# Seven block products instead of eight for the down projection of 24 experts rather than 13, with the outgoing-row buffers shared out anew

## The chip, the cores and the metric

The kernel runs on one core of a Trainium2 chip. The metric is the time of one execution on the device, in microseconds (us). It is the median of several runs.

The core's engines work side by side, each through its own instructions in program order, and semaphores tie them together: TensorE (PE, matrix products; its weight loads are shown apart as PEld), VectorE (DVE), ScalarE (ACT), GpSimd (POOL, which here issues the gathers and scatters of token rows) and SyncE (SP, which issues the plain transfers).

## The reference

The reference is a cross-attention followed by a mixture of experts, on 16 x 128 = 2048 tokens of 512 values:

```python
x = x + xattn(layernorm(x), ctx_512, ctx_512)
h = layernorm(x).reshape(2048, 512)
tidx, tw = gate(h, gate_weight, e_bias)             # 8 of 32 experts for a token
comb = zeros((2048, 32)).at[rows, tidx].set(tw)
g = einsum('td,eid->tei', h, w1)                    # w1, w3: (32, 256, 512)
u = einsum('td,eid->tei', h, w3)
a = silu(g) * u
routed = einsum('tei,edi,te->td', a, w2, comb)      # w2: (32, 512, 256)
shared = silu(h @ sw1.T) * (h @ sw3.T) @ sw2.T
out = x + routed + shared
```

All data are float32. What matters here is the last product of an expert, its down projection: a block of tokens with 256 activations each, times the expert's 256 x 512 matrix `w2`, then scaled by the token's weight for this expert and added to the token's row of the output.

## The kernel before

**The stages.** The first 225 us hold attention, the gate, the routing of tokens to experts and most of the shared expert. The rest, to the end of the span at 863.5 us, goes through the 32 routed experts one after the other. The change lies in this part.

**Places and slices.** `ORDER` lists the experts (by rank of their load), `CAPS` gives each its number of places, and `begins[k]` is the first place of the k-th. All places together are 17664, or 138 slices of 128 (`NS`). For every slice j, GpSimd gathers 128 token rows (`gather`, L1455), VectorE turns them in 32x32 blocks (`transpose`, L1496), and copies (L1493) put the blocks in place as `xall`, tokens along the free dimension.

**Up.** Experts 1 to 30 are `fast`: their up products, for `w1` and `w3`, are made by `seven(k)`, a Winograd scheme that makes a 2x2 block product from seven products (L1598) instead of eight. VectorE makes the sums of weights (L1560), of tokens (L1589) and of products (L1608); ScalarE and VectorE make silu and the product into `acts_of` (`sa`). An expert with over 512 rooms goes in two halves of seven steps each (14 steps); a smaller one in one pass of seven steps.

**Down.** Two ways exist. `down(j)` makes one slice in full: two products of 128x512 a slice (L1739), each shown as two records, into a PSUM tile of its own (`ps_y` or `ps_z`). `evict` then scales it on ScalarE into a row tile `yw` (L1755), and `send_all` has GpSimd scatter it to the output, adding (L1711). A slice that holds places of two experts is sent twice, the second time with the next expert's first send.

`seven_downs(k)` makes four whole slices of one expert at once, as a 2x2 block product of 512 tokens by 512 outputs over 256: seven block products (L1821), each two products of 128x256, into the PSUM pool `ps_p` with its six banks, which the up products use too. It is a generator of eight steps. The first makes four sums on VectorE (L1854); the next seven make one block product each. VectorE makes four more sums of 128x256 and five of 128x512 (both L1812), ScalarE one copy (L1858) and six scalings (L1833). The rows leave in two pair tiles `yp` of two slices each. Its sums lie in the memory of the shared expert's weights (`sup`, `sdn`), one copy of each.

`four_of(k)` decides between the two: it gives the first of four whole slices of expert k, or nothing. Before the change it gives nothing for an even k. So the 13 odd experts from 1 to 25 go through `seven_downs` (52 slices), and the other 86 slices through `down`.

**The order.** All engines but SP run in the order in which the program is written (`manual_schedule`). The main loop goes over half experts (`pieces`), step by step. In every step it first emits the up product, then the jobs that came due (`tick`; `soon(f, after)` puts them on a later step), then a share of the turning, copying and sums by their planned costs, and then so many units of down work as `planned` says: a plain slice weighs 2, a step of `seven_downs` weighs 1. The four first sums of `seven_downs(k)` are emitted three steps into expert k+1; its products follow the units ahead of it, with a rest of four weights kept for the next half.

**Order of sends.** The additions of expert k+1 to the output wait for the landing of those of expert k (`tc.add_manual_dep` in `send`), because both may hold the same token. GpSimd waits in order, and gathers stand behind.

Of the kernel before, what the change touches and what calls it, by code (L numbers as in the profile page):

```python
# [9 lines left out]
F32 = mybir.dt.float32  # L10
# [8 lines left out]
P = 128  # L19
# [27 lines left out]
def tile_xattn_moe(  # L47
# [16 lines left out]
    B, S, D = x.shape  # L64
    E, _, ND, I = w1.shape
# [991 lines left out]
    def experts(ups, in_order, later, products):  # L1057
# [18 lines left out]
        for k in range(E + 1):  # L1076
            r = min(k, E - 1)
# [27 lines left out]
        def load_weights(k, up, down):  # L1105

            r = k % NW
            with tc.issue_after(last[0]) if last else nullcontext():
                _, (e,) = nc.values_load_multi_w_load_instructions(
                    order[0:1, k : k + 1],  # L1110
                    engines=[mybir.EngineType.SP],
                    min_val=0,
                    max_val=E - 1,
                    skip_runtime_bounds_check_because="experts' numbers",
                    bass_reorder=False,
                )
            both = [(wup[r][:, 0], w1), (wup[r][:, 1], w3)] if up else []
            if down:
                both.append((wdn[r], w2))
            for dst, src in both:  # L1120
                dma = nc.sync.dma_start(
                    dst, src[bass.ds(e, 1)].rearrange("o p a b -> (o p) a b")
                )
            last[:] = [dma.ins]
# [317 lines left out]
        def experts_at(j):  # L1442

            for k in range(E):
                a, b = max(begins[k], j * P), min(begins[k + 1], (j + 1) * P)
                if a < b:
                    yield k, a - j * P, b - j * P, a - begins[k]

        xg, yws = {}, {}
# [67 lines left out]
        def soon(f, after=1):  # L1517
            jobs.setdefault(now + after, []).append(f)
# [211 lines left out]
        def down(j):  # L1730
# [19 lines left out]
                    load_weights(ks[0] + NW, False, True)  # L1750
            soon(lambda: evict(j, y))

        def evict(j, y):
            yws[j] = late.tile([P, D], F32, tag="yw", name="yw", bufs=4)
            nc.scalar.activation(yws[j], y, AF.Copy, scale=wt[:, j : j + 1])  # L1755
            send_all(j)

        def send_all(j):
            for args in waiting:
                send(*args)  # L1760
            waiting.clear()
            rows_of = {k: (a, b) for k, a, b, _ in experts_at(j)}
            ks = sorted(rows_of)
            send(j, ks[0], *rows_of[ks[0]])
            waiting.extend((j, k, *rows_of[k]) for k in ks[1:])

        def fast(k):
            return 0 < k < E - 1

        def four_of(k):  # L1770

            if k % 2 == 0 or not fast(k):
                return None
            j = -(-begins[k] // P)
            return j if (j + 4) * P <= begins[k + 1] else None
# [5 lines left out]
        def seven_downs(k):  # L1781


            j = four_of(k)
            first, second = range(j, j + 2), range(j + 2, j + 4)
            col = j * P - begins[k]
            a11, a12, a21, a22 = (
                acts_of[k % NA][:, i, c : c + 2 * P] for c in (col, col + 2 * P) for i in range(NI)
            )
            b11, b12, b21, b22 = (  # L1790
                wdn[k % NW][:, i, c : c + DH] for i in range(NI) for c in (0, DH)
            )
            t1, t2, t3, t4, s1, s2, s4 = (sums_at[:, i] for i in range(7))
            s3 = a21
            p1, u2 = temps_at[:, 0], temps_at[:, 1]
            pending = []

            def then(f, after=1):
                def once():
                    if once in pending:  # L1800
                        pending.remove(once)
                        f()

                pending.append(once)
                soon(once, after)

            def settle():
                for f in list(pending):
                    f()

            def sum_of(to, a, b, op, after=1):
                then(lambda: nc.vector.tensor_tensor(to, a, b, op), after)  # L1812

            def bank():
                return ps_p.tile([P, TB], F32, tag="p", name="y").rearrange(
                    "p (r t) -> p r t", r=2
                )

            def times(acc, a, b, first=True):
                for r in range(2):  # L1820
                    nc.tensor.matmul(  # L1821
                        acc[:, r, :],
                        lhsT=a[:, ts(r, P)],
                        rhs=b,
                        start=(first and r == 0),
                        stop=(r == 1),
                        skip_group_check=not first,
                    )

            def scaled(to, of, js, after):  # L1830
                for r, at in enumerate(js):
                    then(
                        lambda r=r, at=at: nc.scalar.activation(  # L1833
                            to[:, r], of[:, r], AF.Copy, scale=wt[:, at : at + 1]
                        ),
                        after,
                    )

            def sent_out(rows, js, after):
                for r, at in enumerate(js):  # L1840

                    def f(r=r, at=at):
                        yws[at] = rows[:, r, :]
                        send_all(at)

                    then(f, after)

            for to, a, b, op in (
                (s1, a21, a22, ALU.add),
                (s2, s1, a11, ALU.subtract),  # L1850
                (t1, b12, b11, ALU.subtract),
                (t2, b22, t1, ALU.subtract),
            ):
                nc.vector.tensor_tensor(to, a, b, op)  # L1854
            yield
            pa = bank()
            times(pa, a11, b11)
            then(lambda: nc.scalar.copy(p1, pa))  # L1858
            yield
            rows1, rows2 = (late.tile([P, 2, D], F32, tag="yp", name="yp") for _ in range(2))  # L1860
            settle()
            times(pa, a12, b21, first=False)
            scaled(rows1[:, :, 0:DH], pa, first, 1)
            for to, a, b in ((t3, b22, b12), (s3, a11, a21), (s4, a12, s2), (t4, b21, t2)):
                sum_of(to, a, b, ALU.subtract)
            yield
            pb = bank()
            times(pb, s2, t2)
            sum_of(u2, p1, pb, ALU.add)
            yield  # L1870
            pc = bank()
            times(pc, s1, t1)
            sum_of(rows2[:, :, DH:], u2, pc, ALU.add)
            yield
            pd = bank()
            settle()
            times(pd, s3, t3)
            sum_of(rows2[:, :, DH:], rows2[:, :, DH:], pd, ALU.add)
            yield
            times(pc, s4, b22, first=False)  # L1880
            sum_of(rows1[:, :, DH:], u2, pc, ALU.add)
            scaled(rows1[:, :, DH:], rows1[:, :, DH:], first, 3)
            sent_out(rows1, first, 3)
            yield
            settle()
            times(pd, a22, t4, first=False)
            sum_of(rows2[:, :, 0:DH], u2, pd, ALU.add)
            scaled(rows2, rows2, second, 3)
            sent_out(rows2, second, 3)
            if (j + 4) * P == begins[k + 1] and k + NW < E:  # L1890
                load_weights(k + NW, False, True)
            yield
# [3 lines left out]
        def units(j0, j1, ready):  # L1896


            j, of = j0, []
            while j < j1:  # L1900
                ks = [k for k, *_ in experts_at(j)]
                if len(ks) == 1 and four_of(ks[0]) == j:
                    steps = seven_downs(ks[0])
                    jobs.setdefault(ready, []).append(lambda steps=steps: next(steps))
                    of += [(lambda steps=steps: next(steps), ready, 1)] * 7
                    j += 4
                else:
                    of.append((lambda j=j: down(j), ready, 2))
                    j += 1
            return of  # L1910
# [42 lines left out]
        late = ctx.enter_context(tc.tile_pool(name="late", bufs=2, side="right"))  # L1953
# [16 lines left out]
        for n in range(len(pieces)):  # L1970
            k = pieces[n][0]
# [91 lines left out]
    pieces = [(k, i) for k in range(NTB) for i in range(NI)]  # L2063
    left_over = attention_small()
    experts(pieces[1:], in_order, *left_over)
    left = nc.values_load(
        more[0:1, 0:1],
# [63 lines left out]
```

## Time and profile before

| what | value |
|---|---|
| median of 3 runs | 866.39 us (865.27 to 867.35) |
| the profiled execution | 865.3 us; span 863.5 us; mean granted TensorE clock 0.997 |
| busy: PE, DVE, ACT, POOL | 849.7 (98%), 652.6 (76%), 641.2 (74%), 473.5 us (55%) |
| chain that ended last | PE 96%, POOL 2%, ACT 1% |
| down products in that chain | L1739 (plain slices) 16%, L1821 (seven products) 9% |
| scalings into `yw`, L1755 | 86 |
| scalings into `yp`, L1833 | 78 (26 each of three kinds) |
| scatters, L1711 | 98 from `yw`, 52 from `yp` |

How to read it: busy time of an engine is the time covered by its instructions; the records of one engine can overlap by some tens of ns, so the distance from start to start says what an instruction costs in a stream. The chain is followed back from the last instruction, at each step to what released it.

### The profile page before, as it was taken

What the parts mean: (1) busy time and instruction counts of PE and PEld (TensorE: products, weight loads), DVE (VectorE), ACT (ScalarE), POOL (GpSimd) and SP (SyncE); (2) the same over time, 40 slices, a digit from 0 to 9 for tenths busy, and PEclk for the clock granted to TensorE, in tenths of its full rate; (3) what the DMA queues carried; (4) which work ended last, traced back from release to release, by engine and by line L of the source; (5) the groups of instructions that cost most, each with busy time, mean ns of one, the idle gap of its engine ahead of it and who ended that gap; (6) DMA issues with size and microseconds to landing.
All of it is one profiled execution on the core that took longest, in us unless ns stands there. A gap on an engine that the chain in (4) does not pass through costs nothing.

```text
span 863.5 us, 13499 instructions
## 1 busy us (share of the span) xinstructions
PE 849.7 (98%) x4171; PEld 568.3 (66%) x4171; DVE 652.6 (76%) x1593; ACT 641.2 (74%) x1156; POOL 473.5 (55%) x588
## 2 busy tenths in 40 slices
PE   8999999999999999999999999999999999999995
PEld 5344444555766776767686767686778878887763
DVE  7877778858877797778797979797878888867410
ACT  5889741628987797788887979787888888977831
POOL 4487560034545666555646656666564555466554
PEclk9999999999999999999999999999999999999998
DMA  9111111647576888678878878787787788778554
GB/s 293 78 38 49 63 50 44 238 128 214 147 186 128 199 183 215 167 153 188 200 199 159 220 150 224 171 215 166 199 163 203 159 194 204 155 213 164 86 88 57
DMA packets 59873, 137.14 MB, mean 159 GB/s; under 512 B 12168, under 2 KB 16392, under 8 KB 59792
## 3 DMA queue, kind: packets, MB, share of 16 engines
q0 software_dynamic: 32032, 69.25, 42.2%
q1 hardware_dynamic: 27680, 66.81, 23.0%
q8 instruction: 35, 0.57, 0.3%
q14 instruction: 46, 0.38, 0.1%
q10 hardware_dynamic: 80, 0.13, 0.1%
HBM read 96.71 MB, written 46.73 MB: 166 GB/s over the span
## 4 chain that ended last, share of the span: by engine, by line
PE 96%; POOL 2%; issue 1%; ACT 1%; DMA 0%; DVE 0%; POOLq 0%; ACTq 0%
PE p L1598 45%; PE y L1739 16%; PE y L1821 9%; PE gu L285 6%; PE sc L492 5%; PE oT L508 4%; PE y L1392 3%; PE x L462 2%; PE gu L1528 2%; PE tok L1043 1%; POOL out_dram L1711 1%; PE lgT L569 0%; PE lg L584 0%; DMA out_dram<-yw,token 0%; ACT p L502 0%
## 5 line engine op out<-in xcount | busy, mean ns | idle before, releaser
L1493 ACT COPY xall<-blocks 32x512 f32<-32x512 f32 (+4 forms) x684 | 360.4, 527 | 16.3 <-DVE blocks L1496 6.6
L1711 POOL DMA_INDIRECT out_dram<-yw,token x98 | 157.0, 1602 | 138.2 <-DMA out_dram<-yw,token 38.3
L1455 POOL DMA_INDIRECT xgs<-rows,token x138 | 152.8, 1107 | 125.8 <-DVE token L1055 54.2
L1598 PE MATMUL p<-xall,wup 128*128 128x270 f32 (+27 forms) x720 | 185.7, 393 | 0.0
L1598 PEld LDWEIGHTS p<-xall,wup 128*128 128x128 f32 x720 | 136.6, 190 | 38.1 <-issue 10.9
L1739 PE MATMUL y<-wdn,sa 128*128 128x512 f32 (+2 forms) x464 | 161.4, 595 | 0.0
L1598 PE MATMUL p<-t,s 128*128 128x270 f32 (+27 forms) x480 | 123.8, 394 | 0.0
L1711 POOL DMA_INDIRECT out_dram<-yp,token x52 | 85.0, 1635 | 69.2 <-ACT yp L1833 46.4
L1755 ACT ACTIVATE yw<-y,wt 128x512 f32<-128x512 f32 x86 | 58.9, 685 | 72.5 <-PE y L1739 61.1
L1598 PEld LDWEIGHTS p<-t,s 128*128 128x128 f32 x480 | 91.1, 190 | 28.4 <-issue 11.1
L1496 DVE STREAM_TRANSPOSE blocks<-xgs 128x512 f32<-128x512 f32 x138 | 97.2, 705 | 7.7 <-DMA xgs<-rows,token 7.6
L1739 PEld LDWEIGHTS y<-wdn,sa 128*128 128x128 f32 (+2 forms) x464 | 61.4, 162 | 54.7 <-issue 48.2
L1608 DVE TENSOR_TENSOR z<-u,p 128x270 f32<-128x270 f32 (+27 forms) x96 | 48.7, 507 | 42.8 <-PE p L1598 40.2
L502 ACT ACTIVATE p<-sc 128x1024 f32<-128x1024 f32 x64 | 62.1, 1024 | 13.6 <-PE sc L492 13.6
L1598 PE MATMUL p<-t,wup 128*128 128x270 f32 (+27 forms) x240 | 63.8, 396 | 0.0
L1598 PE MATMUL p<-xall,s 128*128 128x270 f32 (+27 forms) x240 | 63.4, 394 | 0.0
L285 PE MATMUL gu<-xall,sup 128*128 128x512 f32 x128 | 59.2, 602 | 0.0
L1598 PEld LDWEIGHTS p<-t,wup 128*128 128x128 f32 x240 | 45.0, 190 | 18.3 <-issue 8.6
L1598 PEld LDWEIGHTS p<-xall,s 128*128 128x128 f32 x240 | 45.3, 190 | 14.3 <-issue 3.1
L1608 DVE TENSOR_TENSOR u<-u,p 128x270 f32<-128x270 f32 (+27 forms) x48 | 24.4, 507 | 30.4 <-PE p L1598 19.4
L492 PE MATMUL sc<-qT,kz 32*128 32x512 f32 x256 | 44.2, 639 | 0.5 <-ACT p L502 0.2
L1589 DVE TENSOR_TENSOR t<-xall,t 128x540 f32<-128x540 f32 (+27 forms) x60 | 43.5, 725 | 1.0
(241 smaller groups left out, 1218.6 us busy)
## 6 DMA issues: line engine op xcount, KB each, us to landing
wup<-in_w_dram SPq DMA_DIRECT2D x64, 512.0 KB
wdn<-in_w_dram SPq DMA_DIRECT2D x32, 512.0 KB
rows<-xn SPq DMA_DIRECT2D x16, 256.0 KB
out_dram<-x SPq DMA_DIRECT2D x16, 256.0 KB
x<-in_x_dram SPq DMA_DIRECT2D x15, 256.0 KB
xgs<-rows,token POOLq DMA_INDIRECT x138
out_dram<-yw,token POOLq DMA_INDIRECT x98
cTs<-in_cT_dram SPq DMA_DIRECT2D x4, 256.0 KB
```

The source lines that it names most:

```text
L285: nc.tensor.matmul(acc, lhsT=sup[:, w, d, ts(i, P)], rhs=xnT[k][:, d, :], start=(d == 0), stop=(d == ND - 1),)
L492: nc.tensor.matmul(scs[j // 2][:, j % 2], lhsT=kzs[b // 4 % 2][rows, b % 4, i, :], rhs=qT[rows], start=True, stop=True, tile_position=(j * ...
L502: nc.scalar.activation(p, sc, AF.Exp, scale=1.0 / HD**0.5)
L1455: nc.gpsimd.indirect_dma_start(out=t, out_offset=None, in_=rows[:, :], in_offset=bass.IndirectOffsetOnAxis(ap=token[:, j : j + 1], axis=0) ...
L1493: yield on_ACT, 1 + many, lambda dst=dst, of=of, copy=copy: copy(dst, of)
L1496: nc.vector.transpose(blocks[:, j % NB_BUF, :], xgs[:, j % NG_BUF, 0:D])
L1598: nc.tensor.matmul(acc[:, i, 0:h], lhsT=w[:, i, d, :], rhs=x[:, d, :], start=(first and i == d == 0), stop=(i == outs[-1] and d == 1), ski ...
L1608: soon(lambda: nc.vector.tensor_tensor(out_, a, b, ALU.add))
L1711: ins = nc.gpsimd.indirect_dma_start(out=flat, out_offset=bass.IndirectOffsetOnAxis(ap=token2[:, k - 1 : k] if a else token[0:b, j : j + 1 ...
L1739: nc.tensor.matmul(y[c0:c1, :], lhsT=acts_of[k % NA][:, i, col : col + c1 - c0], rhs=wdn[k % NW][:, i, :], start=(i == 0), stop=(i == NI - 1),
L1755: nc.scalar.activation(yws[j], y, AF.Copy, scale=wt[:, j : j + 1])
L1821: nc.tensor.matmul(acc[:, r, :], lhsT=a[:, ts(r, P)], rhs=b, start=(first and r == 0), stop=(r == 1), skip_group_check=not first,)
```

## The change

Three edits. `four_of` no longer refuses an even k, so every fast expert with four whole slices takes `seven_downs`. By the table of `begins` these are experts 1 to 3 and 5 to 25, 24 in all; expert 4 has only three whole slices, and from 26 on there are too few. New are 2, 6, 8, 10, 12, 14, 16, 18, 20, 22 and 24. The plain slices fall from 86 to 42: 20 up to slice 87, and the last 22, slices 116 to 137.

`yw` goes from four buffers to two, and `yp` from two to three, so the memory is the same: 16 KB a partition.

`row_tile(j)` chooses the tile of a plain slice: while an expert with four whole slices is still to come, a `yw`; after that, one half of a pair tile. So the last 22 slices have six rows to turn over.

```diff
+        spare = []
+
+        def row_tile(j):
+            if any(four_of(k) is not None for k in range(experts_at(j).__next__()[0], E)):
+                return late.tile([P, D], F32, tag="yw", name="yw", bufs=2)
+            if not spare:
+                two = row_tiles()
+                spare.extend(two[:, r, :] for r in range(2))
+            return spare.pop(0)
+
+        def row_tiles():
+            return late.tile([P, 2, D], F32, tag="yp", name="yp", bufs=3)
+
         def evict(j, y):
-            yws[j] = late.tile([P, D], F32, tag="yw", name="yw", bufs=4)
+            yws[j] = row_tile(j)
...
         def four_of(k):
-            if k % 2 == 0 or not fast(k):
+            if not fast(k):
                 return None
...
-            rows1, rows2 = (late.tile([P, 2, D], F32, tag="yp", name="yp") for _ in range(2))
+            rows1, rows2 = row_tiles(), row_tiles()
```

## The prediction

> **What bounds the kernel now.** I read the page first: busy shares and the chain that ended last.
>
> ```profile
> span 863.5 us, 13499 instructions
> ...
> PE 849.7 (98%) x4171; PEld 568.3 (66%) x4171; DVE 652.6 (76%) x1593; ACT 641.2 (74%) x1156; POOL 473.5 (55%) x588
> ...
> PE 96%; POOL 2%; issue 1%; ACT 1%; DMA 0%; DVE 0%; POOLq 0%; ACTq 0%
> ```
>
> TensorE is 96% of the chain. A busy engine can still wait, so I read its timeline, start to start, for the two kinds of down product.
>
> ```profile
> 458.00 1.88 PE L1739 MATMUL y<-wdn,sa 128*128 128x512 f32 x4
> 459.72 1.07 PE L1598 MATMUL p<-t,wup 128*128 128x270 f32 x4
> ...
> 483.76 1.03 PE L1821 MATMUL y<-sup 128*128 128x256 f32 x4
> 484.62 1.98 PE L1598 MATMUL p<-t,s 128*128 128x270 f32 x8
> ```
>
> A plain slice (four records) takes 459.72 - 458.00 = 1.72 us, 429 ns a record; a block product (four records) 0.86 us, 216 ns. Both go with the columns, and nothing stands between: over all experts I find hardly a start later than that. So work taken from TensorE here is time, as long as nobody else falls behind. Who could, the windows of single experts tell (expert 10, 11; 21 to 26), each row with the window, its length, and the busy time of PE, PEld, DVE, ACT and POOL:
>
> ```profile
> 418.70:441.00 22.30, 22.30 (x93) 14.76 (x92) 16.71 (x42) 19.42 (x38) 14.95 (x12) 1.00 0.83 191
> 441.00:460.60 19.60, 19.60 (x81) 15.19 (x80) 17.80 (x42) 15.17 (x27) 10.96 (x8) 1.00 0.71 175
> ...
> 646.40:665.30 18.90, 18.90 (x82) 15.22 (x81) 16.43 (x35) 14.83 (x26) 9.16 (x7) 1.00 0.74 190
> 665.30:683.10 17.80, 17.80 (x77) 14.30 (x76) 14.88 (x36) 14.59 (x31) 7.47 (x6) 1.00 0.66 142
> 683.10:701.70 18.60, 18.60 (x81) 15.22 (x81) 16.22 (x35) 17.71 (x38) 12.80 (x10) 1.00 0.95 235
> 701.70:719.40 17.70, 17.70 (x78) 14.45 (x77) 14.95 (x37) 14.67 (x27) 7.54 (x5) 1.00 0.68 155
> 719.40:737.80 18.40, 18.40 (x81) 15.19 (x80) 15.89 (x36) 14.51 (x31) 13.89 (x12) 1.00 0.86 205
> 737.80:755.20 17.40, 17.40 (x78) 14.47 (x77) 14.54 (x37) 16.41 (x37) 7.28 (x5) 1.00 0.75 172
> ```
>
> VectorE is second, at 75 to 91%, against 76% on the page, and the change gives it work.
>
> **The change part by part.**
>
> TensorE. Each of the 11 new experts loses 4 x 4 records of 429 ns = 6.86 us and gains 28 of 216 ns = 6.05 us: -0.82 us, or -9.0 us for eleven. Against this speaks a rule of the Trainium skill: "TensorE: Matmul & The Clock Gate", section "The mechanism", says that a weight load overlaps with running matmuls only when it goes to another row group, and every load here fills all 128 rows. Then the 190 ns loads of the trace would be paid: 28 x 406 - 16 x 619 = +1.46 us an expert, +16 us in all. But the rows above show four block products in 0.86 us, loads included. I take -9.0.
>
> VectorE. `evict` cost it nothing; `seven_downs` gives it eight sums of 128x256 and five of 128x512. In this stream small sums start 0.33 us apart:
>
> ```profile
> 478.68 0.42 DVE L1812 TENSOR_TENSOR sup<-wdn 128x256 f32<-128x256 f32 x1
> 479.01 0.42 DVE L1812 TENSOR_TENSOR sa<-sa 128x256 f32<-128x256 f32 x1
> 479.35 0.42 DVE L1812 TENSOR_TENSOR sup<-sa,sup 128x256 f32<-128x256 f32 x1
> ```
>
> A 512 sum costs 0.60 us in the same way. So 8 x 0.34 + 5 x 0.60 = 5.7 us an expert, 63 us in all, none of it on the path while VectorE has room. "VectorE: DVE Perf Modes", section "The DRAIN you can't avoid", says that the next operation does not start until the pipe is empty; by whole records it would be 8 x 0.42 + 5 x 0.685 = 6.8 us. The starts above lie inside the record before, so I take 5.7 and keep 6.8 for the range.
>
> Where it falls: by the planner's order, an expert's eight small sums and one or none of the large land in the window of the next expert (3.3 us), the rest in the one after (2.4 us). Window 11 then holds 17.8 + 3.3 = 21.1 us of VectorE beside 19.6 - 0.8 = 18.8 us of TensorE: 2.3 us too much. Window 12 has 22.2 us, 16.56 of it busy (same table), takes 2.4 and has 3.2 us left to catch up. So it goes for 13, 15, 17 and 19 too. Windows 21 to 26 have no such rest: 92.9 us busy (sum of the six rows) + 3 x 5.7 = 110.0, beside 108.8 - 3 x 0.82 = 106.3 us: VectorE is 3.7 us late at the end. What does lateness cost? The trace shows one case:
>
> ```profile
> 762.73 0.68 DVE L1812 TENSOR_TENSOR yp<-yp,y 128x512 f32<-128x512 f32 x1
> 766.87 0.71 DVE L1496 STREAM_TRANSPOSE blocks<-xgs 128x512 f32<-128x512 f32 x1 [3.45 <-DMA xgs<-rows,token]
> ...
> 767.64 0.65 DVE L1608 TENSOR_TENSOR z<-z,p 128x480 f32<-128x480 f32 x1
> ```
>
> A gather held VectorE for 3.45 us, the addition `z` behind it ran some 4 us after its product, and in TensorE's timeline of that stretch no start is late. So 3.7 us late is near what is known to be free, in experts of one pass. In those of two halves the most I find is 3.3 us after the start of a step, at the begin of expert 5. There TensorE next wants a `ps_p` bank that an addition has to free two steps (2 x 1.4 us) after it was due. I take 1.0 us of stall for windows 11 to 20 (0 to 5 x 0.8) and 1.5 us for 21 to 27 (0 to 4). At 6.8 us an expert, the late sum grows by 3 x 1.1 and the stall with it, inside these ends.
>
> ScalarE. Six scalings and a copy for four evictions: 0.48 + 4 x 0.40 + 2 x 0.63 = 3.3 us, start to start, against 4 x 0.585 = 2.3: +1.0 us an expert. The pair of windows 10 and 11 has 7.3 us idle. Zero; if that cover were gone, 11 us.
>
> The two `yw` tiles. Where plain slices stay single, two are enough. Slices 18 to 22 stay five in a row:
>
> ```profile
> 333.40 1.63 POOL L1711 DMA_INDIRECT out_dram<-yw,token x1 [3.92 <-DMA out_dram<-yw,token]
> 335.33 1.79 POOL L1711 DMA_INDIRECT out_dram<-yw,token x1 [0.31 <-issue]
> ...
> 335.29 0.69 ACT L1755 ACTIVATE yw<-y,wt 128x512 f32<-128x512 f32 x1 [0.88 <-PE y L1739]
> ```
>
> At 333.40 slice 19 is sent for the second time, after a wait for the landing of the send issued at 326.72, 6.7 us before. The eviction of slice 21 at 335.29 will need 19's tile, free at about 333.4 + 6.7 = 340.1: ScalarE stands up to 4.8 us, and behind it stand three copies into `xall`, a silu and the next eviction. ScalarE is idle 4.7 us in this window, and two banks are still free when the next half starts. I take 1.0 us (0 to 4.8).
>
> The three pair tiles. Rows 2 of an expert take over rows 1 of the one before. Its first write, on VectorE, comes nine steps or more (13 us) after that send, in one-pass experts five steps of 2.5 us. A send lands within 6.7 us, its pair another 2 us on. Zero, up to 1.5 us for each of five one-pass experts. The last 22 slices get six rows for four, so nothing is later there.
>
> GpSimd and queues. The number of scatters is the same, 150. They are issued in bursts of two with gathers behind, but an expert's rows now all leave before the next one's, where today's waits for the place before are 38.3 us on `yw` and 21.9 us on `yp` (waits of GpSimd). Zero to me: GpSimd is busy 55%. SP loads the next `wdn` at the same place, after the fourth slice, three experts ahead; also zero.
>
> Sum: -9.0 + 1.0 + 1.5 + 1.0 = -5.5 us. The profiled execution took 865.3 us, 1.8 over its span and 1.1 under the median 866.39. From it 859.8, from the median 860.9; I forecast the latter.
>
> **The rivals.**
>
> 1. *All covered.* TensorE keeps its pace and all of 9.0 us comes: 857.4. For it: no late start today, 3.45 us of lateness free. Against it: the balance of VectorE, below zero in eleven windows.
>
> 2. *VectorE becomes the bound in every window for itself*, slower. If lateness can't be carried into the next expert, because the additions free `ps_p` banks within the step in which TensorE wants them, each odd window grows by 3.3 us less its idle time: for 11, 13, 15, 17 and 19 about 3.3 - 1.6 = 1.7 each, 8.3 us; in 21 to 26 about 0.2 each, 1.2 us. TensorE's saving lies in the same windows and is lost, but for those of 2 and 6, 1.6 us: 866.4 + 9.5 - 1.6 = 874. It decides when VectorE's lateness over a fraction of a step stops TensorE. Against it: expert 27 above.
>
> 3. *Nothing left.* The stalls eat the gain: VectorE's additions are late, ScalarE's scalings wait for them in order, its copies and silus behind them come late, and VectorE waits for the copies. Each pass costs about a step of 1.4 us in six or seven windows: 866.
>
> 4. *It doesn't do what it says* (fewer than 24 experts): excluded by `begins`; 52 scatters from `yp` today are 13 x 4, as it should be.
>
> **How the numbers follow.** Gain with some stall, 858.5 to 864.6: 0.47. All covered, under 858.5: 0.25. Nothing left, 864.7 to 868.1: 0.11, of it 0.09 within 0.2% (1.7 us, about what a measurement of this kernel can tell from no change) and 0.02 slower. Slower by rival 2, or by a longer hold on ScalarE or at a pair tile: 0.17. So faster 0.72, same 0.09, slower 0.19. Time 860.9; range 857.0 to 869.0, which leaves out some 0.03 below and 0.15 above.
>
> **What would show it.** L1821 with 672 records and L1739 with 176 fewer, each at 216 and 429 ns: else the first term is wrong. VectorE busy near 652.6 + 63, ScalarE near 652. In windows 11 to 19 VectorE without a gap, and TensorE's timeline with starts late by under 1 us, each after a VectorE addition. One wait of an eviction L1755 for a scatter near 335 us, some 4 us long. Waits of GpSimd for scatters below 60 us. I am wrong if TensorE's idle time and late starts sum to over 9 us, or if weight loads come out of cover.

## The result, and the profile after

The changed kernel takes 876.54 us (median of 4 runs, 874.89 to 878.63), against 865.95 before in the same comparison: ratio 1.012, 95% interval 1.0101 to 1.014. It is slower by 1.2%, and outside the range of the prediction (857.0 to 869.0).

In the changed kernel's profile the line numbers behind L1755 shift: the scaling of a plain slice L1755 is now L1769, VectorE's sums L1812 are L1826, the seven products L1821 are L1835, the scalings L1833 are L1847, the copy of `p1` L1858 is L1872. From its page, the span, the busy times and the chain that ended last:

```profile
span 875.7 us, 13959 instructions
...
PE 849.3 (97%) x4303; PEld 593.8 (68%) x4303; DVE 711.0 (81%) x1736; ACT 648.6 (74%) x1189; POOL 477.0 (54%) x588
...
DMA 10%; issue 6%; POOL 5%; DVE 4%; ACT 2%; PE 1%; POOLq 0%; DVEq 0%; ACTq 0%
```

The shares of the chain add to only 28% of the span: it could be followed back to 635 us and no further. In that part TensorE has 1%, and sends, their landings and VectorE release one another; before, TensorE had 96% of the whole span. The busy time of TensorE hides more than it tells: 849.3 us is almost that of before, though there is less work. About 3 us of it are records that last longer at a lower granted clock. The rest is lateness that the records cover: a record of a block product lasts 379 ns, but the next one may start after 216, so a start up to 0.16 us late leaves no idle time.

The span grew by 12.2 us. 10.1 of them lie in the experts' stage, from the first L1598 product to the end of TensorE's last product (629.1 us before, 639.2 after). 1.7 lie ahead of it, where the profiled run had the clock at 0.62 and 0.53 in two windows from 120 us on, and the run before had 1.00 with the same work. That part is most likely chance, not the change: of the twelve profiles of the experiments below, one shows it too (`e7_light`), the others not.

The windows of experts 10, 11 and 21 to 23 (columns as in the prediction):

```profile
421.20:444.40 23.20, 22.58 (x102) 16.21 (x101) 19.98 (x49) 19.83 (x41) 8.30 (x6) 1.00 0.55 150
444.40:464.10 19.70, 19.02 (x85) 15.89 (x84) 19.46 (x49) 15.93 (x29) 12.71 (x11) 1.00 0.81 187
654.70:672.70 18.00, 18.00 (x86) 15.95 (x85) 17.63 (x41) 14.64 (x27) 9.78 (x8) 1.00 0.63 162
672.70:695.40 22.70, 20.27 (x86) 16.96 (x85) 18.86 (x42) 16.56 (x35) 16.30 (x12) 0.92 0.86 200
695.40:713.10 17.70, 17.70 (x85) 15.95 (x84) 17.33 (x38) 16.59 (x37) 10.12 (x8) 1.00 0.78 179
```

Windows 21 and 23 are 0.9 us shorter (18.90 and 18.60 before), about what the products save. Window 11 is 0.1 us longer than before instead, with VectorE busy 99% of it, window 10 is 0.9 us longer, and window 22 is 4.9 us longer. The waits (us in total, times, the longest) name what stands in between; the first row is of the kernel before, the others are of the changed one:

```profile
ACT yp L1833 <- DVE yp L1812: 7.3, 6, 3.4
...
ACT yp L1847 <- DVE yp L1826: 46.4, 24, 5.7
...
PEld y L1835 <- ACT sdn L1872: 17.4, 17, 2.7
...
PE y L1835 <- ACT sdn L1872: 10.6, 14, 2.4
...
ACT yw L1769 <- DMA out_dram<-yw,token: 7.0, 2, 4.4
...
DVE yp L1826 <- DMA out_dram<-yp,token: 4.9, 2, 3.2
```

ScalarE waits over six times as long as before for VectorE's sums, with not twice as many scalings that need them, and TensorE waits for ScalarE's copy of `p1`. This is the read of bank `pa` between its two products: the first is copied out, and the second (the record `y<-wdn,sa` after `pa`'s first, one step later) may add to the bank only after that. Adding up every product of full rows that starts more than 0.15 us after its predecessor allows, I find 16.7 us in the experts' stage, against none before: 12.9 behind this copy (14 places), 2.0 behind VectorE's read of `pc` before `pc`'s second product, 0.2 elsewhere, and 1.6 in records at a low clock. Smaller lateness grew by another 2.4. So 9.0 saved, 19.1 lost, +10.1.

Two of those places show what makes the copy late. The first is where slice 21 leaves (ScalarE's timeline, then TensorE's):

```profile
340.62 0.69 ACT L1769 ACTIVATE yw<-y,wt 128x512 f32<-128x512 f32 x1 [4.36 <-DMA out_dram<-yw,token]
...
346.82 0.57 ACT L1872 COPY sdn<-y 128x512 f32<-128x512 f32 x1
```

```profile
347.44 1.13 PE L1835 MATMUL y<-wdn,sa 128*128 128x256 f32 x4 [1.50 <-ACT sdn L1872]
```

ScalarE stood 4.36 us at the single tile, ran without a gap from then on, and its copy came late. The second is the worst, in window 22 (VectorE's, ScalarE's and TensorE's timelines):

```profile
678.97 0.69 DVE L1826 TENSOR_TENSOR yp<-sdn,y 128x512 f32<-128x512 f32 x1 [3.19 <-DMA out_dram<-yp,token]
```

```profile
685.95 0.91 ACT L1847 ACTIVATE yp<-yp,wt 128x256 f32<-128x256 f32 x2 [5.73 <-DVE yp L1826]
...
689.53 0.58 ACT L1872 COPY sdn<-y 128x512 f32<-128x512 f32 x1
```

```profile
690.16 1.77 PE L1835 MATMUL y<-wdn,sa 128*128 128x256 f32 x4 [2.36 <-ACT sdn L1872]
```

The third pair tile isn't free: VectorE stands 3.19 us for a scatter that GpSimd issued at 672.14. That scatter left late (ScalarE's timeline, then GpSimd's):

```profile
664.46 0.91 ACT L1847 ACTIVATE yp<-yp,wt 128x256 f32<-128x256 f32 x2 [2.78 <-DVE yp L1826]
```

```profile
662.44 1.76 POOL L1711 DMA_INDIRECT out_dram<-yp,token  x1 [0.30 <-issue]
...
670.22 1.62 POOL L1711 DMA_INDIRECT out_dram<-yp,token  x1 [1.66 <-DMA out_dram<-yp,token]
672.14 1.58 POOL L1711 DMA_INDIRECT out_dram<-yp,token  x1 [0.30 <-issue]
```

The rows were scaled by 665.4. They were sent at 670.22 and 672.14, behind three gathers and the landing of the send of 662.44, which belongs to the expert before. All of VectorE's sums move back, ScalarE's scaling waits for one of them, six copies into `xall` and a silu stand behind that scaling, and the copy of `p1` behind these. The windows after it show a second price, the granted clock, third from the end of a row:

```profile
688.00:690.00 2.00, 0.00 (x0) 0.00 (x0) 1.97 (x4) 1.95 (x5) 1.70 (x2) 1.00 0.61 67
690.00:692.00 2.00, 1.84 (x5) 1.55 (x6) 2.00 (x6) 1.93 (x6) 1.69 (x2) 0.63 0.83 104
692.00:694.00 2.00, 2.00 (x6) 1.59 (x6) 2.00 (x7) 1.98 (x5) 1.39 (x3) 0.52 0.91 189
```

### The profile page after: what moved, and what is told of

It reads as the page before. It is cut to its first block, busy times and chain, and to the rows that moved or that the text cites. A ratio compares the mean times of both kernels' runs of the same rounds, so it can differ in the third digit from the quotient of the medians.

```text
span 875.7 us, 13959 instructions
## 1 busy us (share of the span) xinstructions
PE 849.3 (97%) x4303; PEld 593.8 (68%) x4303; DVE 711.0 (81%) x1736; ACT 648.6 (74%) x1189; POOL 477.0 (54%) x588
## 5 line engine op out<-in xcount | busy, mean ns | idle before, releaser
L1711 POOL DMA_INDIRECT out_dram<-yp,token x122 | 199.9, 1639 | 159.5 <-ACT yp L1847 67.9
L1598 PE MATMUL p<-xall,wup 128*128 128x270 f32 (+27 forms) x720 | 185.9, 394 | 0.0
L1598 PEld LDWEIGHTS p<-xall,wup 128*128 128x128 f32 x720 | 136.8, 190 | 31.4 <-issue 4.7
L1598 PE MATMUL p<-t,s 128*128 128x270 f32 (+27 forms) x480 | 123.7, 394 | 0.0
L1598 PEld LDWEIGHTS p<-t,s 128*128 128x128 f32 x480 | 91.2, 190 | 20.0 <-issue 3.2
L1847 ACT ACTIVATE yp<-yp,wt 128x256 f32<-128x256 f32 (+1 forms) x96 | 53.8, 607 | 47.1 <-DVE yp L1826 46.4
L1739 PE MATMUL y<-wdn,sa 128*32 128x512 f32 (+2 forms) x288 | 78.7, 597 | 0.0
L1711 POOL DMA_INDIRECT out_dram<-yw,token x28 | 45.3, 1619 | 53.7 <-DMA out_dram<-yw,token 28.5
L1598 PE MATMUL p<-t,wup 128*128 128x270 f32 (+27 forms) x240 | 64.9, 402 | 0.0
L1598 PE MATMUL p<-xall,s 128*128 128x270 f32 (+27 forms) x240 | 63.6, 396 | 0.1
L1835 PE MATMUL y<-wdn,sa 128*128 128x256 f32 x192 | 51.5, 392 | 10.6 <-ACT sdn L1872 10.6
L1598 PEld LDWEIGHTS p<-t,wup 128*128 128x128 f32 x240 | 45.9, 194 | 15.3 <-DVE z L1608 2.9
L1826 DVE TENSOR_TENSOR yp<-sdn,y 128x512 f32<-128x512 f32 x72 | 49.1, 682 | 8.5 <-DMA out_dram<-yp,token 4.9
L1598 PEld LDWEIGHTS p<-xall,s 128*128 128x128 f32 x240 | 45.2, 190 | 13.5 <-issue 3.7
L1835 PEld LDWEIGHTS y<-wdn,sa 128*128 128x128 f32 x192 | 35.4, 191 | 22.4 <-ACT sdn L1872 17.4
L1835 PE MATMUL y<-sup,sa 128*128 128x256 f32 x192 | 49.4, 380 | 0.0
```

Source lines behind the costliest of these rows:

```text
L1598: nc.tensor.matmul(acc[:, i, 0:h], lhsT=w[:, i, d, :], rhs=x[:, d, :], start=(first and i == d == 0), stop=(i == outs[-1] and d == 1), ski ...
L1711: ins = nc.gpsimd.indirect_dma_start(out=flat, out_offset=bass.IndirectOffsetOnAxis(ap=token2[:, k - 1 : k] if a else token[0:b, j : j + 1 ...
L1739: nc.tensor.matmul(y[c0:c1, :], lhsT=acts_of[k % NA][:, i, col : col + c1 - c0], rhs=wdn[k % NW][:, i, :], start=(i == 0), stop=(i == NI - 1),
L1835: nc.tensor.matmul(acc[:, r, :], lhsT=a[:, ts(r, P)], rhs=b, start=(first and r == 0), stop=(r == 1), skip_group_check=not first,)
L1847: lambda r=r, at=at: nc.scalar.activation(to[:, r], of[:, r], AF.Copy, scale=wt[:, at : at + 1]),
```

## The experiments

Three theories stood at the start. **A**: order; the copy of `p1` is late because it stands on ScalarE behind scalings that wait for VectorE. **B**: load; VectorE has too much to do, and TensorE stops wherever that comes out. **C**: tiles; three pair tiles and two single ones are too few when experts of seven products follow each other. "Late" below is the same sum of late starts as above. The time before was 865.22 to 865.25 us in all these comparisons. The medians are of four or five runs, if nothing else is said, whose times spread over 0.2 to 7.1 us, so a difference of 1 or 2 us between two experiments says little.

**1. `e1_pb_first`: order alone.** The product into a new bank, `pb`, goes ahead of the second one into `pa`, so that the copy of `p1` has two steps.

```diff
             times(pa, a11, b11)
             then(lambda: nc.scalar.copy(p1, pa))
             yield
+            pb = bank()
+            times(pb, s2, t2)
+            for to, a, b in ((t3, b22, b12), (s3, a11, a21), (s4, a12, s2), (t4, b21, t2)):
+                sum_of(to, a, b, ALU.subtract)
+            yield
             rows1, rows2 = row_tiles(), row_tiles()
             settle()
             times(pa, a12, b21, first=False)
             scaled(rows1[:, :, 0:DH], pa, first, 1)
-            for to, a, b in ((t3, b22, b12), (s3, a11, a21), (s4, a12, s2), (t4, b21, t2)):
-                sum_of(to, a, b, ALU.subtract)
-            yield
-            pb = bank()
-            times(pb, s2, t2)
             sum_of(u2, p1, pb, ALU.add)
```

> The changed kernel with one edit: in seven_downs the third block product (pb) goes before the second product into pa, so that ScalarE's copy p1 of pa has one step more before TensorE writes pa again. Same instructions, same sums. Theory A (TensorE stands because that copy comes late, ScalarE standing in order at row scalings that wait for VectorE): the 12.9 us of late starts at L1835 behind ScalarE's copy fall below 3 us, the clock drop near 690 us goes with them, and the time falls from 876.5 to 862 to 867. Theory B (VectorE's load is the bound, the copy only the place where it shows): TensorE stalls move to other products, time 873 or more.

871.07 us (867.48 to 873.34), ratio 1.0057 (1.0038 to 1.0076): between what A and B expected. The waits for the copy are gone, and half of the loss has only moved. Waits, then VectorE's and TensorE's timelines at the largest new stop:

```profile
DVE yp L1826 <- DMA out_dram<-yp,token: 14.4, 7, 3.6
...
PEld y L1835 <- DVE yp L1826: 10.6, 9, 3.1
```

```profile
465.53 0.69 DVE L1826 TENSOR_TENSOR yp<-sdn,y 128x512 f32<-128x512 f32 x1 [3.28 <-DMA out_dram<-yp,token]
```

```profile
466.27 1.86 PE L1835 MATMUL y<-wdn,sup 128*128 128x256 f32 x4 [2.61 <-DVE yp L1826]
```

With the first stop out of the way the pair tiles hold VectorE more often (7 times for 2), and now the second product into `pc` pays.

**2. `e2_no_force` and `e12_both`: the scalings' place in the order.** `settle()` brings forward all work that is still deferred; here scalings and sends (deferred by three steps) keep their three steps. `e12_both` has this and the edit of 1.

```diff
             def then(f, after=1):
...
+                if after > 1:
+                    soon(f, after)
+                    return
                 pending.append(once)
```

> The changed kernel with one edit: settle() brings forward only sums and copies due after one step; the scalings and sends that are due after three steps stay there. So ScalarE meets the rows' scalings one or two steps later, when VectorE has made the rows. Theory A: ScalarE's waits for VectorE's yp fall from 46 us to under 25, the copies p1 come earlier, and the time falls to 868 to 873 (the scalings of the second pair, just ahead of the next copy, are not moved). Theory B: no change, 875 to 878. Theory C (the three pair tiles are the cause): slower, since the tiles are held longer, 878 or more.

> Both edits, of e1 and of e2, in the changed kernel. Theory A: as e1 or up to 2 us better, 860 to 866, below the kernel before. Theory B: 873 or more. Theory C: between 870 and 878, with VectorE waiting for scatters of yp.

884.79 (ratio 1.0249, 1.0211 to 1.0287) and 879.59 us (1.0175, 1.0158 to 1.0192). ScalarE's waits for VectorE at the scalings fell from 46.4 to 24.7 us, and yet the late starts behind the copy were 14.8 us: so shorter waits at the scalings did not bring the copy forward. What did grow is VectorE's wait for a pair tile, to 14.3 us (longest 5.9) and 16.7 us: rows that are scaled later are sent later, and the tile comes free later. That is the way C expected, and `e12_both` is slower still than it said. As this edit also holds the tiles longer, it does not settle A by itself.

**3. `e4_load`: load alone.** The kernel before, with 17 additional sums of 128x256 on VectorE, whose results nobody uses, for each of 11 even experts (2 to 24 without 4), spread over the steps where the change would have its sums. Nothing else is changed.

```diff
+        def extra_sums(k, ready):
...
+            for at, n in zip(after, (4, 4, 2, 2, 2, 2, 1)):
+                jobs.setdefault(ready + at, []).append(lambda n=n: sums(n))
```

> The kernel before, with VectorE loaded as by the change but nothing else: for each of the 11 experts 17 extra sums of 128x256 (5.7 us) into a free block, at the steps where the change has its sums; the results are not used. Down products, ScalarE's work and buffers stay as before. Theory A: VectorE's lateness alone reaches TensorE hardly, since plain slices have no copy in front of their products: 866 to 868. Theory B: 870 or more.

875.97 us, ratio 1.0124 (1.0108 to 1.0141): as slow as the whole change, with no tile or product touched (VectorE is busy 718.4 us here, 711.0 in the changed kernel). Late: 6.3 us in the up products, where the second product into a bank waits for VectorE's `z` (about 0.5 to 1.0 each in experts 8, 10, 12 and so on), 2.4 behind the copy, 0.7 behind VectorE's read of `pc`. So VectorE's lateness does stop TensorE, in this stage too, which the prediction had taken as nearly free.

**4. `e7_light`: the change without its load.** The eight small sums and `u2` of all 24 experts run over 32 columns; the other columns are left out.

```diff
-                nc.vector.tensor_tensor(to, a, b, op)
+                nc.vector.tensor_tensor(to[:, 0:32], a[:, 0:32], b[:, 0:32], op)
...
-                sum_of(to, a, b, ALU.subtract)
+                sum_of(to[:, 0:32], a[:, 0:32], b[:, 0:32], ALU.subtract)
...
-            sum_of(u2, p1, pb, ALU.add)
+            sum_of(u2[:, :, 0:32], p1[:, :, 0:32], pb[:, :, 0:32], ALU.add)
```

> The changed kernel, with every instruction kept but VectorE's eight small sums and the sum u2 of all 24 experts run over 32 of their 128x256 columns only; the other columns of these operands are left out, so part of the down result isn't computed. VectorE's busy time should fall by 24 x (8 x 0.25 + 0.4) = some 55 us to about 655 us, as in the kernel before, while order, waits, ScalarE's work, buffers and sends stay as in the changed kernel. Theory A (the copy p1 comes late because it stands on ScalarE behind scalings: a matter of order): late starts after that copy stay at 8 us or more, 868 us or more. Theory B (VectorE's load is the cause): the copy p1 is in time and all of the 9 us comes, 856 to 860 us. Theory C (three pair tiles, with their waits for scatters): the waits of VectorE for a pair tile stay, one stall of some 3 us with the slow clock after it, 862 to 866 us.

866.5 us (median of 20 runs, 864.31 to 872.88), ratio 1.0017 (1.0004 to 1.003), VectorE busy 663.0 us, 48.0 less than in the changed kernel. 10.0 us come back, but not the saving: 8.0 us are still late. 2.2 are at slice 21, 2.2 at and behind the pair tile in window 22, and the rest are some ten places of 0.2 to 0.8 us, nearly all behind the copy. No theory alone fits; C's range (862 to 866) comes nearest.

**5. `e8b_four_only`: tiles alone.** Four pair tiles, no single ones (the same 16 KB); a plain slice takes a row of one.

```diff
         def row_tile(j):
-            if any(four_of(k) is not None for k in range(experts_at(j).__next__()[0], E)):
-                return late.tile([P, D], F32, tag="yw", name="yw", bufs=2)
-            if not spare:
-                ...
-            return spare.pop(0)
+            return row_tiles()[:, 0, :]
...
-            return late.tile([P, 2, D], F32, tag="yp", name="yp", bufs=3)
+            return late.tile([P, 2, D], F32, tag="yp", name="yp", bufs=4)
```

> The changed kernel with four pair tiles in place of three pair tiles and two single ones (the same 16 KB); a plain slice takes one row of a pair tile. Theory C: waits of VectorE for a scatter at a pair tile (4.9 us, two times) vanish, and with them the stall at expert 22 and its slow clock, about 4.8 us; 871 to 872 us. Theories A and B: the other sixteen late starts stay as they are, so no better than 871; if VectorE's lateness is what holds TensorE everywhere, its wait at expert 22 only hands the stall to a later one, 873 to 876.

868.93 us, ratio 1.0045 (1.003 to 1.0061): 7.6 us below the change, more than C's 4.8, and slice 21's stop went too. The single and the pair tiles change together here, so the 7.6 us are not split between them. No wait of VectorE or ScalarE for a scatter is left; 9.7 us are late behind the copy.

**6. `e8_four_pairs`: order and tiles.** The edits of 1 and 5 together.

> Both single repairs at once: the product into pb ahead of the second one into pa (as in the earlier experiment, 871.07), and four pair tiles. Theory C: waits of VectorE at a pair tile (14.4 us there) vanish, late starts of the second product into pc fall from 8.2 us to under 4, 865 to 867 us. Theory B (load): VectorE stays behind TensorE in the windows of two halves, so late starts after its sums remain at 6 us or more, 868 to 871 us. Below 864 us only if neither load nor tiles were the cause.

860.06 us (859.61 to 860.61), ratio 0.9936 (0.9921 to 0.9951): faster than both kernels, though VectorE does all its added work. The expectation had "below 864 only if neither load nor tiles were the cause"; that was wrong: with the full load, the two repairs are worth 5.5 and 7.6 us alone and 16.5 together. The page, and windows 10, 11, 21 and 22 of this kernel:

```profile
span 858.8 us, 13940 instructions
...
PE 843.7 (98%) x4303; PEld 593.7 (69%) x4303; DVE 709.5 (83%) x1736; ACT 650.9 (76%) x1189; POOL 477.0 (56%) x588
...
PE 67%; DVE 11%; ACT 8%; issue 6%; DMA 5%; POOL 3%; POOLq 0%; DVEq 0%; ACTq 0%
```

```profile
417.10:439.40 22.30, 22.30 (x101) 16.29 (x100) 19.78 (x52) 19.62 (x40) 7.97 (x7) 1.00 0.60 162
439.40:458.80 19.40, 19.12 (x86) 15.90 (x85) 19.16 (x47) 15.84 (x29) 9.92 (x8) 1.00 0.65 162
643.00:661.00 18.00, 18.00 (x85) 15.94 (x84) 17.11 (x39) 14.99 (x27) 9.52 (x8) 1.00 0.72 178
661.00:678.90 17.90, 17.90 (x86) 15.99 (x85) 17.76 (x41) 14.44 (x31) 12.40 (x9) 1.00 0.85 213
```

In windows 11 and 22 VectorE is busy 99% of the time, and TensorE stands idle 0.3 us in the one and not at all in the other. VectorE is late in this kernel as well: ScalarE's scalings wait 39.7 us for its sums, 22 times. It only has more room before TensorE needs what it is late with. In all, 3.1 us are late.

**7. `e14_light_four` and `e15_light_both`: the light load in 5 and in 6.**

> Four pair tiles and the changed kernel's order of products, with VectorE's nine small operations of each expert over 32 columns only (the other columns of these operands are left out, so part of the down result isn't computed). The same light work with three pair tiles took 866.5, with late starts of 2.2 us at slice 21's single tile and of 2.2 us at a pair tile. Theory now (load and tiles each add lateness, and the second product into pa, one step after the first, turns it into stops): both of these go, about 861 to 862.5 us. Rival, load alone with tiles that only hand the lateness on: 865 to 867.

> Four pair tiles, the product into pb ahead of the second into pa, and VectorE's nine small operations of each expert over 32 columns only (the other columns left out, so part of the down result isn't computed). It is the floor for this structure: what the full load still costs in 860.06 us with both repairs. Theory now: that load is nearly covered, the late starts of 3.1 us there are all that it costs, so 856.5 to 858 us, the 9 us of the product records and nothing else. Rival, load still the bound in VectorE's gapless windows: well below that, under 855, which the sum of TensorE's records doesn't allow.

860.65 us (ratio 0.9945, 0.9926 to 0.9965) and 856.46 us (0.989, 0.9873 to 0.9907). Both lie just under the lower end of what was expected. In the first 3.2 us are late, all behind the copy, without the load and without a wait for a tile; ScalarE's scalings still wait 17.2 us for VectorE there. In the second nothing is late, and the time is 8.8 us below the kernel before. The runs make a table (us):

| VectorE's small sums | products | tiles | time |
|---|---|---|---|
| full | as changed | 3 pairs, 2 single | 876.54 |
| full | `pb` first | 3 pairs, 2 single | 871.07 |
| full | as changed | 4 pairs | 868.93 |
| full | `pb` first | 4 pairs | 860.06 |
| light | as changed | 3 pairs, 2 single | 866.5 |
| light | as changed | 4 pairs | 860.65 |
| light | `pb` first | 4 pairs | 856.46 |

The load costs 10.0 us in the changed kernel, 8.3 with four pair tiles, 3.6 with both repairs. The first two are too near each other to be told apart, the third is not. So it is no fixed price: the order, with tiles enough, sets what a late VectorE costs. The light load with `pb` first and the old tiles was not run.

**8. `e10_few`: a few more experts, old buffers.** The kernel before, with experts 2, 6 and 20 added.

```diff
-            if k % 2 == 0 or not fast(k):
+            if (k % 2 == 0 and k not in (2, 6, 20)) or not fast(k):
```

> The kernel before, its own buffers, with the seven products for experts 2, 6 and 20 added to its thirteen odd ones. In the changed kernel the windows after these three were 0.84 us shorter each, and the windows behind those not longer than before but for 6 (1.8 us, behind 4 and 5). Theory B: VectorE has room there, so it gains 3 x 0.82 = 2.5 us, 862.5 to 864 us. Theory A (the order of ScalarE's work behind any expert of seven products): each new expert costs as much as it gains, 865 to 867 us.

884.18 us, ratio 1.0209 (1.0195 to 1.0223): a miss for both theories. I had left the pair tiles out. With two of them the second pair of an expert takes the tile of the second pair of the one right before it, and waits for that to land (sent at 304.24 and 306.12). VectorE's and TensorE's timelines, and the windows from 310 us on:

```profile
314.29 0.69 DVE L1812 TENSOR_TENSOR yp<-sdn,y 128x512 f32<-128x512 f32 x1 [5.21 <-DMA out_dram<-yp,token]
```

```profile
315.03 2.07 PE L1821 MATMUL y<-wdn,sup 128*128 128x256 f32 x4 [5.65 <-DVE yp L1812]
```

```profile
312.00:314.00 2.00, 0.00 (x0) 0.00 (x0) 0.00 (x0) 0.00 (x0) 0.00 (x0) 0.50 1.04 388
314.00:316.00 2.00, 0.97 (x2) 0.83 (x3) 1.71 (x5) 0.00 (x0) 0.00 (x0) 0.50 0.60 246
316.00:318.00 2.00, 2.00 (x6) 1.36 (x5) 1.97 (x4) 1.64 (x4) 1.00 (x1) 0.50 0.21 28
```

Three such stops (13.4 us), the low clock after them (6.5 us) and 1.0 us behind a copy are more than the whole loss of 18.9; the saving goes against them.

**9. `e6_bufs`: the changed buffers on the kernel before.** The changed kernel, with `four_of` refusing even experts again.

> The kernel before with the changed kernel's buffers only: three pair tiles, two single tiles while experts of seven products are to come; seven products for odd experts as before. If the prediction's term for the two single tiles holds (ScalarE up to 4.8 us at slice 21 and at every plain expert's third slice), 866 to 869 us; if ScalarE's room covers it, 864.5 to 866. The three pair tiles can't cost here, as experts of seven products never follow each other.

950.95 us, ratio 1.1001 (1.0963 to 1.1039). I expected 869 at most. Here the even experts' plain slices, four or so in a row, go through two single tiles:

```profile
ACT yw L1769 <- DMA out_dram<-yw,token: 104.3, 27, 10.0
...
PE y L1835 <- ACT sdn L1872: 58.3, 12, 8.1
```

Each such wait holds ScalarE, and again the copy of `p1` and the second product into `pa` are what it holds up. After the long stops TensorE runs on at a low clock (0.966 on the mean, for 0.997 before). The change leaves only 20 such scalings of single tiles, and only slices 18 to 22 come five in a row: two waits.

**10. `e11_pool`: VectorE's load given to GpSimd.** The kernel of 6, with the four sums of weights of each expert on GpSimd.

```diff
-            def sum_of(to, a, b, op, after=1):
-                then(lambda: nc.vector.tensor_tensor(to, a, b, op), after)
+            def sum_of(to, a, b, op, after=1, eng=None):
+                then(lambda: (eng or nc.vector).tensor_tensor(to, a, b, op), after)
...
-                nc.vector.tensor_tensor(to, a, b, op)
+                of_weights = nc.gpsimd if any(to is t for t in (t1, t2)) else nc.vector
+                of_weights.tensor_tensor(to, a, b, op)
...
-                sum_of(to, a, b, ALU.subtract)
+                sum_of(to, a, b, ALU.subtract, eng=nc.gpsimd if any(to is t for t in (t3, t4)) else None)
```

> Both repairs (860.06 us), and the four sums of weights of each expert (t1 to t4, 128x256) given from VectorE to GpSimd, where such a sum takes 0.74 us: VectorE loses 24 x 4 x 0.34 = 33 us, GpSimd gains 71 us of 381 free ones. If VectorE's load is what is left: 857 to 858.5. Rival: GpSimd stands in front of sends, for scatters 67.5 us and for scalings 45 us in all, up to 7.8 us at once, and t1 and t2 are wanted three steps (4 us) after they are asked for, so the products into pb and pc come late in many experts: 866 to 885.

920.37 us, ratio 1.0629 (1.0595 to 1.0664): the way the rival said, and far above its range. The sums take what they should (0.74 us), but stand behind sends. GpSimd's timeline, then TensorE's, and the wait in all (us, times, the longest):

```profile
440.27 1.57 POOL L1711 DMA_INDIRECT out_dram<-yp,token  x1 [5.53 <-DMA out_dram<-yp,token]
446.12 1.73 POOL L1711 DMA_INDIRECT out_dram<-yp,token  x1 [4.28 <-issue]
...
451.12 0.74 POOL L1821 TENSOR_TENSOR sup<-wdn 128x256 f32<-128x256 f32 x1
```

```profile
451.91 2.08 PE L1830 MATMUL y<-sup,sa 128*128 128x256 f32 x4 [6.78 <-POOL sup L1821]
```

```profile
PEld y L1830 <- POOL sup L1821: 47.6, 10, 7.6
```

## Why the prediction was wrong

**The saving, -9.0 us: right.** A block product and what follows it still start 0.86 us apart, loads hidden; with every stop gone (`e15_light_both`) the time is 8.8 us below the kernel before. The page of the Trainium skill that the prediction weighed against it ("TensorE: Matmul & The Clock Gate", section "The mechanism") also says that a load is pulled ahead when it goes to the background weight buffer, which the prediction left out; no run here tells which case this is.

**VectorE's work, 63 us: right in size.** Its busy time rose by 58.4 us (652.6 to 711.0), 5.3 us an expert for the 5.7 taken. The 6.8 us of the rule on the drain would have made 75; that section of the Trainium skill ("VectorE: DVE Perf Modes", section "The DRAIN you can't avoid") also says that a next operation that is not held starts earlier, and the prediction's rows show it, 0.33 us apart in records of 0.42. ScalarE's busy time rose by 7.4 us for the 11 taken.

**What VectorE's lateness costs, 1.0 + 1.5 us: the step that failed.** Taking the small sums off VectorE gives back 10.0 us in the changed kernel (experiment 4), and such sums alone add 10.7 us to the kernel before (experiment 3). The prediction took the tolerance from expert 27, where 4 us of lateness cost nothing, and from a `ps_p` bank that is wanted two steps later. Both readings miss what TensorE needs soonest. These are its products around that lateness, in the kernel before:

```profile
763.37 1.03 PE L1821 MATMUL y<-wdn,sup 128*128 128x256 f32 x4
...
765.86 1.03 PE L1821 MATMUL y<-sup,sa 128*128 128x256 f32 x4
...
768.35 1.89 PE L1598 MATMUL p<-t,wup 128*128 128x240 f32 x8
```

The two block products of the scheme are the last ones in that stretch, and VectorE had read their banks by 763.4, before it stood. The up product at 768.35 is the one that adds to the bank which the late `z` reads, and `z` (767.64, 0.65 us long) ended 0.06 us before it. So 4 us were not a sample of what is free; they were all that was free, in steps of 2.5 us. In a block product the bank to which TensorE adds again comes sooner: `pa` one step after its first product, behind a copy on ScalarE that stands behind scalings that wait for VectorE (46.4 us, 7.3 before), and `pc` two steps after; an up bank has three or four. Experiments 1, 3 and 6 show it from three sides. The prediction's own sign of being wrong, over 9 us of idle time and late starts, came with 19.1; most of these starts follow ScalarE's copy, and not a VectorE addition as it had named.

**ScalarE, +1.0 us an expert, "zero": wrong by up to 3.2 us.** So much is late behind the copy of `p1` with a light VectorE and four pair tiles (experiment 7), and none of it with the copy given one step more. How much of it is ScalarE's own work, and how much its remaining waits for VectorE, isn't separated. Idle time over a window says nothing of one copy that is due within a step.

**The single tiles, 1.0 us (0 to 4.8): within its range.** ScalarE waited twice where one wait was forecast, 2.67 us at 333.03 and 4.36 us at 340.62, near the place named, and TensorE started 1.67 us late behind the second.

**The pair tiles, zero to 1.5 us for each of five: the second step that failed.** The sum of the prediction has nothing for them. Tiles of both kinds together cost 7.6 us alone and 11.0 with `pb` first (871.07 to 860.06). The prediction counted steps from one expert's send to the next one's write as if the send came on time. It doesn't: the rows in the tile that was wanted in window 22 were scaled by 665.4 and left at 670.22 and 672.14, behind gathers and the landing of the send before. The scatter itself took the 6.7 us that the prediction has, to 678.8; VectorE was ready at 675.8 and began at 678.97. The low clock after a stop, 1.6 us, was in no term.

**GpSimd's waits for scatters, under 60 us: right** (31.4 on `yw` and 26.2 on `yp`, as far as the profile names what ended a wait).

**The rivals.** Rival 2 came nearest in time (874), and its point of decision, that VectorE's lateness over a fraction of a step stops TensorE, is what the runs show. But its mechanism, VectorE as the bound in every window for itself, is not: with the same load `e8_four_pairs` takes 860.06. The path of the worst stop is that of rival 3 (VectorE late, scalings wait, copies late), which priced all its stalls at 9 us (857.4 to 866); the runs have 20.1 between the changed kernel and `e15_light_both`. What stays open: how the 12.9 us behind the copy split between scalings that waited and ScalarE's other work; the runs vary both at once. Open, too, is how the tiles' share splits between single and pair tiles.

## What to carry to other kernels

When work is moved from the bound engine to one with room, look for the shortest way back: the place where the bound engine needs a result of the other soonest, such as a second product into a bank that has to be read first; the tolerance found elsewhere in the trace doesn't count there, and lateness that cost nothing may have cost nothing by a hair. Before such a move, give that place a step more (another independent product in between) and count the outgoing tiles from the time a send is really issued, not from when it is due. Shares of busy time over a window would have refused `e8_four_pairs`, in which VectorE is 99% busy in windows 11 and 22 and the kernel still gains 0.6%.

## What the runs showed of the hardware

A short pause of TensorE can cost more than itself. After the stop of 2.36 us at 690.16 the granted clock was 0.63 and 0.52 for two windows of 2 us; after one of 5.65 us (`e10_few`) it was 0.50 to 318 us, 3 us into the new work. But it need not. In `e12_both` a stop of 2.86 us left the clock at 1.00 (TensorE's timeline, then the window after it):

```profile
596.71 1.13 PE L1838 MATMUL y<-wdn,sup 128*128 128x256 f32 x4 [2.86 <-DVE yp L1829]
```

```profile
598.00:600.00 2.00, 2.00 (x10) 1.59 (x9) 1.93 (x6) 0.00 (x0) 0.00 (x0) 1.00 0.37 117
```

Over the experts' stage of all fourteen profiles, twelve stops last 1.9 to 3.0 us, and six of them bring a low clock: one of 1.95 us does (`e11_pool`, to 738.34), one of 2.36 us doesn't (`e6_bufs`, to 304.88). All eighteen stops of over 4 us bring it. The low stretches last 3.4 us, or two or three times that. The Trainium skill, "TensorE: Matmul & The Clock Gate", section "Part 1: The HAM clock gate", puts the drop at an idle window of about 3.4 us, and says that windows run freely. The length of the low stretches and the chance in the short stops agree with free windows of that length. That a whole one must be idle does not hold here: 2.36 us sufficed, and near 120 us a stretch in which TensorE was busy 1.15 of 2 us had a low clock after it in two profiles (`after`, `e7_light`) and not in the one of before.
